# A four-layer graph attention kernel: the first head's G made by TensorE, and another order for first pieces, masks and elu

## The chip, the cores and the metric

The kernel runs on one core of one Trainium2 chip. The core has a matrix engine (TensorE, in the profile PE, with its weight loads as PEld), a vector engine (VectorE, DVE), a scalar engine (ScalarE, ACT), a general engine (GpSimd, POOL), and a queue of transfers that SyncE issues (SP). Each runs its own list of instructions in order and waits for the others through semaphores. The metric is the device time of one execution, in microseconds (us).

## The reference

The input x has 16 batch entries of 1024 nodes with 256 features, and adj is one 1024 x 1024 graph for all of them. Four layers follow one another, each of the form x = x + gnn(relu(layernorm(x))). Layers 0 and 2 have four heads of 64 features, layers 1 and 3 have one head of 256. For one head, cut to what matters:

```python
h    = relu(layernorm(x));  wh = h @ W
e    = leaky_relu(wh @ a_src [:, None] + wh @ a_dst [None, :])   # slope 0.2, in layer 3 0.01
e    = where(adj > 0 (layers 0, 1) or adj != 0 (layers 2, 3), e, -inf)
x    = x + elu(softmax(e) @ wh)                                   # layer 3: relu
```

## The kernel before, in words

**Algebra.** The exponential of a leaky relu of a sum is a maximum of two products, each with one factor by row and one by column. So no 1024 x 1024 exponential is computed. With a factor G for the node that receives and a factor r for the node that sends, DVE makes the unnormalised weights of 128 senders against all 1024 receivers in one instruction: w = max(G, r) * mask (`weights`, L355). G has to stand in PSUM as a row of 1024 values, the same on all 128 partitions. The other factors are folded into wh (`project`, L314), and one more column of wh gives the softmax denominator.

**Steps.** One layer of one batch entry is a step; there are 64. Four entries are under way at a time (streams), and the order of steps (`order_of_steps`) alternates four-head and one-head steps, except at the two ends: steps 0, 1 and 2 all have four heads, steps 5 and 6 are both of one head, 59 and 60 are both of four heads, and 61, 62 and 63 of one.

**What a step does.** Its preparation (`preparation`) is a list of 21 pieces:

- 0 to 4: statistics on DVE (L238), their combination on POOL (L265 to L277), normalisation on ACT (L283).
- 5 to 16: for each half of the nodes, transposes on PE (L291) with relu on ACT (L292), and projections on PE (L302), each evicted from PSUM by ACT (L304). The fourth of each half is followed by exponentials (L310, L312) and the fold on POOL (L314).
- 17 `factors`: gcol, the G of each node, by two ACT instructions (L320, L321).
- 18 `rows`: PE turns gcol into rows (L326), ACT copies them (L328), and SP writes them to DRAM (grow).
- 19 `fetch_heads`: SP reads a head's row back from DRAM into gs on all 128 partitions (L344). Two gs buffers are there.

Just before it is needed, `broadcast` copies gs into PSUM by ACT (L350). Then come 8 weights instructions per head, and the aggregation on PE (`aggregate`, L371) in 8 groups per step: in a four-head step a group is 128 matmuls of width 65, in a one-head step 16 of width 257. ACT evicts each group (L386). 18 buffers hold w. PSUM banks for projections, transposes and groups come from one pool of four, in turn.

`finish` closes a step: the reciprocal of the denominators (`divide`), scaling and the min of elu (`scaled`), the exponential on ACT (L420), and the sum into x (L426 on DVE, L427 on POOL). In `scaled` POOL multiplies (L414). The min is done by DVE ahead of it (L413) where the next step has one head, else by POOL behind it (L416).

**What sets the order.** The program order is written out by the kernel itself. Time is counted in slots, eight per step, one per group. The lists FOUR, SHORT, ONE, SOON, FIRST, TIGHT and LATE give the slot of each of the 21 pieces relative to a step's start. At each slot the main loop emits the group, then those pieces of the previous step's finish that are due (list `at`), then due preparation pieces, then weights ahead of time. `free` is the slot in which the stream's x is ready again. An engine does its instructions in this order, so an instruction that waits holds all behind it on its engine.

**The start.** The adjacency arrives as int32 rows in eight blocks. DVE turns a block into signs (L194), PE transposes it into PSUM (`turn`, L208), DVE writes the mask of layers 0 and 1 (`positive`, L211), and ACT the mask of layers 2 and 3 as a square (`nonzero`, L215). Blocks 0 to 3 share PSUM tiles in pairs, out of the pool that G uses later. A list named `order` mixes these pieces with step 0's preparation.

Of the kernel before, what the change touches and what calls it, by code (L numbers as in the profile page):

```python
# [35 lines left out]
P = 128  # L36
EPS = 1e-5
SHIFT = 60.0
STREAMS = 4
# [8 lines left out]
FOUR = (-8, -8, -5, -3, -2, -1, -1, 0, 0, 0, 0, 0, 0, 2, 2, 2, 2, 3, 8, 8, 10)  # L48
SHORT = (-4, -4, -4, -2, -2, -1, -1, 0, 0, 0, 0, 0, 0, 2, 2, 2, 2, 3, 8, 8, 10)
ONE = (2, 2, 2, 4, 4, 5, 5, 6, 6, 6, 6, 6, 6, 8, 8, 8, 8, 8, 10, 10, 12)  # L50
SOON = (0, 0, 0, 1, 2, 3, 3, 4, 4, 5, 5, 5, 5, 6, 6, 7, 7, 8, 9, 9, 11)
FIRST = (-4, -4, -4, -2, 0, -1, -1, -1, -1, -1, -1, 1, 1, 2, 2, 2, 2, 2, 3, 3, 5)
TIGHT = (5, 5, 5, 7, 7, 8, 8, 9, 9, 9, 9, 9, 9, 10, 10, 10, 10, 10, 11, 11, 13)
LATE = (0, 0, 0, 1, 1, 2, 2, 3, 3, 3, 3, 3, 3, 4, 4, 4, 4, 5, 6, 6, 8)


# [9 lines left out]
def kernel(ctx: ExitStack, tc: tile.TileContext, x, adj, ws, avs, out):  # L66
# [273 lines left out]

    def fetch(n, h):

        gs = state[n]["gs", h] = work.tile([P, N], F32, name="gs", bufs=2)
        nc.sync.dma_start(out=gs, in_=state[n]["grow"][h].rearrange("c i -> (c i)")  # L344
                          .partition_broadcast(P))

    def broadcast(n, h):

        g = state[n]["g", h] = ps_g.tile([P, N], F32, name="g")
        nc.scalar.activation(g, state[n]["gs", h], AF.Copy)  # L350

    def weights(n, h, jc):
# [6 lines left out]
    def aggregate(n, h, i0, per):  # L359
# [25 lines left out]
            return  # L385
        nc.scalar.activation(st["y"][:, i0:i0 + per, h, :], acc, AF.Copy)  # L386

    def finish(n):

        b, l = steps[n]  # L390
        H = LAYERS[l][0]
        D = F // H
        st = state[n]

        def views(half):
            s = slice(half * HALF, (half + 1) * HALF)
            return (xs[b][:, s, :].rearrange("p c (h d) -> p (c h) d", h=H),
                    st["y"][:, s, :, 0:D].rearrange("p c h d -> p (c h) d"),
                    st["r"][:, s, :].rearrange("p c h -> p (c h)"))

        def divide():
            st["r"] = small.tile([P, C, H], F32, name="r")
            nc.vector.reciprocal(st["r"], st["y"][:, :, :, D])

        def scaled(half):
            xh, yh, r = views(half)
            rb = r[:, :, None].to_broadcast([P, HALF * H, D])
            time = LAYERS[steps[n + 1][1]][0] == 1
            if l < L - 1:

                e = st["e", half] = prep.tile([P, HALF * H, D], F32, name="e")
                if time:
                    nc.vector.scalar_tensor_tensor(e, yh, 0.0, rb, op0=ALU.min, op1=ALU.mult)  # L413
            nc.gpsimd.tensor_tensor(yh, yh, rb, op=ALU.mult)  # L414
            if l < L - 1 and not time:
                nc.gpsimd.tensor_scalar(e, yh, 0.0, -3.0e38, op0=ALU.min, op1=ALU.max)  # L416

        def exponential(half):
            if l < L - 1:
                nc.scalar.activation(st["e", half], st["e", half], AF.Exp)  # L420

        def add(half):
            xh, yh, r = views(half)
            if l < L - 1:
                e = st["e", half]
                nc.vector.scalar_tensor_tensor(e, e, -1.0, yh, op0=ALU.add, op1=ALU.max)  # L426
                nc.gpsimd.tensor_add(xh, xh, e)  # L427
                return
            nc.vector.scalar_tensor_tensor(xh, yh, 0.0, xh, op0=ALU.max, op1=ALU.add)  # L429

        def store(half):
            nc.sync.dma_start(
                out=out[b].rearrange("(p c) f -> p c f", p=P)[:, half * HALF:(half + 1) * HALF],
                in_=xs[b][:, half * HALF:(half + 1) * HALF, :])
            if half == 1 and b + STREAMS < B:
                load(b + STREAMS)


        at = (0, 0, 0, 0, 1, 1, 1) if H > 1 else (0, 0, 1, 1, 2, 2, 3)
        return list(zip(at, (divide, lambda: scaled(0), lambda: scaled(1), lambda: exponential(0),  # L440
                             lambda: exponential(1), lambda: add(0), lambda: add(1)))) + (
                    [(4, lambda: store(0)), (4, lambda: store(1))] if l == L - 1 else [])
# [15 lines left out]
    def prepare(upto):  # L458

        while agenda and agenda[0][0] <= upto:  # L460
            _, n, piece, last = agenda.pop(0)
            piece()
            if last:
                done["prepared"] = n + 1
# [37 lines left out]
    last, agenda_of = {}, []  # L502
    for n, (b, l) in enumerate(steps):

        free = 8 * (last[b % STREAMS] + 1) + (8 if l == 0 else 2) if b % STREAMS in last else -99
        last[b % STREAMS] = n
        start = 8 * (n - 2) + (n == 3)
        kind = (ONE if n < len(steps) - 2 else TIGHT) if LAYERS[l][0] == 1 else SOON if n < 5 else FOUR
        if kind is FOUR and free > start + kind[0]:
            kind = SHORT  # L510
        if free > start + kind[0]:
            kind = LATE
            start = max(free, agenda_of[-1][0] + 5, start - LATE[7])
        agenda_of.append([start + k for k in kind] if n > 1 else FIRST)
        if n > 2:

            assert agenda_of[n][7] >= 8 * (n - 2)
            was = agenda_of[n - 1]
            assert agenda_of[n][3] >= was[5] and agenda_of[n][4] >= was[11]
    ending = []  # L520
    later = {}
    with tc.manual_schedule():
        blocks = [mask_rows(c) for c in range(C)]
        layer = [weight_columns(l) for l in range(L)]
        layer[0][0](nc.scalar)
        load(0, 2)
        load_weights(0)
        for c in range(C):
            blocks[c][0]()
        load(1)  # L530
        load_weights(1)
        for i in range(2, STREAMS):
            load(i)
        nc.scalar.activation(warm, half1, AF.Exp)
        nc.vector.tensor_copy(identb, ident)
        layer[0][1]()
        first = [piece for _, piece in preparation(0)]

        order = (

            [first[0], first[1], first[3], lambda: layer[0][2](range(1)), first[2],
             lambda: layer[0][2](range(1, K)), first[5], first[6], first[4], layer[0][3]]

            + [blocks[c][1] for c in range(4)]
            + [first[7], first[8], blocks[0][2], blocks[4][1], blocks[5][1], blocks[0][3],
               first[9], first[10], blocks[1][2], blocks[0][4], blocks[6][1], blocks[7][1],
               blocks[1][3], first[11], first[12], blocks[2][2], blocks[1][4],
               lambda: prepare(-4), first[13], first[14], blocks[3][2], blocks[2][4],
               blocks[2][3], blocks[3][3], first[15], first[16]]

            + [first[17], blocks[4][2], blocks[5][2], first[18], first[19],
               blocks[4][3], blocks[3][4], blocks[4][4], blocks[5][3], blocks[5][4],
               blocks[6][2], blocks[7][2], blocks[6][3], blocks[6][4], blocks[7][3], blocks[7][4]])
        plan(1)
        planned = 2
        for piece in order:
            piece()
        done["prepared"] = 1
        emit_tiles(C // 2, must=True)
        prepare(-2)  # L560
        emit_tiles(C, must=True)
        prepare(-1)
        for i in range(2, STREAMS):
            load_weights(i)

        for l, at in ((1, 1), (2, 8 * 3 + 3), (3, 8 * 5 + 3)):
            for i, piece in zip((0, 1, 2, 8), layer[l]):
                later[at + i] = piece
        for n in range(len(steps)):
            for k, (h, i0, per) in enumerate(groups(n)):  # L570
                while planned < len(steps) and min(
                        a[0] for a in agenda_of[planned:planned + 2]) <= 8 * n + k:
                    plan(planned)
                    planned += 1
                emit_tiles(place[n, h, C - 1] + 1, must=True)
                aggregate(n, h, i0, per)
                if i0 + per == C:
                    done["free"] = place[n, h, C - 1] + 1
                while ending and ending[0][0] <= k:
                    ending.pop(0)[1]()  # L580
                upto = min(done["tiles"] + (6 if per > 1 else 3), done["free"] + WBUFS)
                emit_heads(upto - 1)
                if 8 * n + k in later:
                    later[8 * n + k]()
                prepare(8 * n + k)
                emit_tiles(upto)
            for _, piece in ending:
                piece()
            ending = finish(n) if n < len(steps) - 1 else []
# [35 lines left out]
```

## Time and profile before

| what | us |
|---|---|
| median of 3 runs (lowest, highest) | 2562.08 (2561.59, 2566.2) |
| span of the profiled execution | 2559.7 |
| TensorE busy | 2497.2 |
| VectorE busy | 2018.9 |
| ScalarE busy | 1130.0 |
| GpSimd busy | 1110.1 |
| first weights instruction (L355) begins | 37.96 |
| step 3's aggregation begins | 201.19 |

A line of the summary gives an engine's busy time, its share of the span and the number of its instructions. In a line of the order of time, the columns are start, duration, engine, line, operation, written tile <- read tiles, and in brackets how long the engine stood idle before and which instruction released it. In a line of the waits they are who waited <- for whom: total, number, longest. A busy PE is not PE at its peak, since matmuls are pipelined.

### The profile page before, as it was taken

The numbers are of one execution on the slowest core, as the hardware profiler recorded it, in microseconds if no ns is written. First come the engines' busy times: TensorE is split into PE (matmuls) and PEld (weight loads), VectorE is DVE, ScalarE is ACT, GpSimd is POOL, SyncE is SP. The second block draws the span as 40 slices with busy tenths as digits, with TensorE's granted clock in tenths as the row PEclk, the third lists the DMA queues.
The fourth block names the chain that finished last, engine by engine and source line by source line (L and its number), as shares of the span: only waits on it lengthen the run. The fifth ranks groups of instructions, "written<-read, shape, count | busy, mean of one in ns | idle before, by whom it ended". The sixth has DMA issues, their size and how long they took to land.

```text
span 2559.7 us, 88174 instructions
## 1 busy us (share of the span) xinstructions
PE 2497.2 (98%) x40088; PEld 2258.7 (88%) x40088; DVE 2018.9 (79%) x2140; ACT 1130.0 (44%) x2502; POOL 1110.1 (43%) x1364
## 2 busy tenths in 40 slices
PE   6899999999999999999999999999999999999899
PEld 5788889999989999989999889999888999998887
DVE  8888578888778888778888778888778878778863
ACT  5344454434444444544434544444444444543331
POOL 3244455533444544544433545543443444544341
PEclk8999999999999999999999999999999999999999
DMA  5101010121212110111221101111212210111101
GB/s 182 52 28 41 12 43 35 44 77 44 76 42 70 44 44 11 43 41 71 77 76 44 43 35 44 44 44 43 75 37 76 76 36 19 43 35 43 61 10 58
DMA packets 36991, 129.01 MB, mean 50 GB/s; under 512 B 6278, under 2 KB 9094, under 8 KB 34696
## 3 DMA queue, kind: packets, MB, share of 16 engines
q1 hardware_dynamic: 36606, 123.36, 13.7%
q8 instruction: 314, 5.14, 0.8%
q14 instruction: 61, 0.50, 0.1%
q10 hardware_dynamic: 10, 0.00, 0.0%
HBM read 105.91 MB, written 17.43 MB: 48 GB/s over the span
## 4 chain that ended last, share of the span: by engine, by line
PE 84%; DVE 9%; POOL 3%; issue 2%; ACT 2%; DMA 0%; DVEq 0%; POOLq 0%; ACTq 0%
PE bank L371 63%; PE bank L302 17%; DVE w L355 7%; PE bank L291 4%; DVE bn L238 1%; ACT xn L283 1%; POOL x L427 1%; POOL rstd L271 1%; DVE e L426 0%; PE bank L326 0%; POOL y L414 0%; DVE e L413 0%; POOL e L416 0%; ACT g L350 0%; DMA x<-in_x 0%
## 5 line engine op out<-in xcount | busy, mean ns | idle before, releaser
L371 PE MATMUL bank<-whx,w 128*64 128x65 f32 x36864 | 1909.5, 241 | 29.3 <-DVE w L355 17.6
L371 PEld LDWEIGHTS bank<-whx,w 128*64 128x64 f32 x36864 | 1745.1, 145 | 174.3 <-DVE w L355 24.3
L355 DVE SCALAR_TENSOR_TENSOR w<-g,rcol,mask 128x1024 f32<-128x1024 f32 x1280 | 1540.2, 1272 | 392.1 <-PE bank L371 314.3
L386 ACT ACTIVATE y<-bank 128x260 f32<-128x260 f32 (+1 forms) x504 | 193.9, 385 | 1090.9 <-PE bank L371 1090.9
L414 POOL TENSOR_TENSOR y<-y,r 128x1024 f32<-128x1024 f32 x126 | 263.4, 2100 | 579.7 <-DVE e L413 448.6
L314 POOL TENSOR_TENSOR whx<-whx 128x1024 f32<-128x1024 f32 x128 | 257.5, 2012 | 583.9 <-ACT whx L312 583.9
L302 PE MATMUL bank<-wx,hT 128*128 128x264 f32 (+1 forms) x2048 | 482.2, 388 | 5.6 <-ACT y L386 4.4
L302 PEld LDWEIGHTS bank<-wx,hT 128*128 128x128 f32 x2048 | 382.7, 191 | 76.2 <-ACT y L386 14.4
L427 POOL TENSOR_TENSOR x<-x,e 128x1024 f32<-128x1024 f32 x96 | 247.9, 2593 | 136.1 <-DVE e L426 135.0
L283 ACT ACTIVATE xn<-x,shift,rstd 128x256 f32<-128x256 f32 x512 | 264.6, 590 | 73.2 <-POOL shift L277 71.2
L304 ACT ACTIVATE whx<-bank 128x264 f32<-128x264 f32 (+1 forms) x512 | 188.7, 384 | 178.3 <-PE bank L302 177.8
L238 DVE BATCH_NORM_STATS2 bn<-x 128x6 f32<-128x256 f32 x512 | 175.9, 411 | 79.5 <-POOL x L427 76.2
L426 DVE SCALAR_TENSOR_TENSOR e<-e,y 128x1024 f32<-128x1024 f32 x96 | 154.1, 1623 | 37.3 <-ACT e L420 30.0
L350 ACT ACTIVATE g<-gs 128x1024 f32<-128x1024 f32 x160 | 163.6, 1023 | 12.1 <-DVE w L355 9.7
L291 PE MATMUL bank<-ident,xn 128*128 128x128 f32 x1024 | 137.9, 277 | 10.5 <-ACT xn L283 10.3
L291 PEld LDWEIGHTS bank<-ident,xn 128*128 128x128 f32 x1024 | 120.8, 142 | 27.7 <-ACT xn L283 14.6
L292 ACT ACTIVATE hT<-bank 128x512 f32<-128x512 f32 x256 | 136.7, 585 | 1.4 <-PE bank L291 1.2
L271 POOL TENSOR_TENSOR rstd<-rstd,neghalf 128x4 f32<-128x4 f32 (+1 forms) x97 | 120.2, 1239 | 15.1 <-DVE shift L272 7.6
L420 ACT ACTIVATE e<-e 128x1024 f32<-128x1024 f32 x96 | 100.7, 1049 | 23.4 <-POOL e L416 23.1
L413 DVE SCALAR_TENSOR_TENSOR e<-y,r 128x1024 f32<-128x1024 f32 x60 | 72.5, 1250 | 2.2
L429 DVE SCALAR_TENSOR_TENSOR x<-y,x 128x1024 f32<-128x1024 f32 x30 | 44.9, 1499 | 2.0 <-POOL y L414 2.0
L312 ACT ACTIVATE whx<-whx,nbias 128x16 f32<-128x16 f32 (+1 forms) x128 | 40.2, 314 | 4.2
(63 smaller groups left out, 442.1 us busy)
## 6 DMA issues: line engine op xcount, KB each, us to landing
gs<-grow SPq DMA_DIRECT2D x160, 512.0 KB
x<-in_x SPq DMA_DIRECT2D x15, 1024.0 KB
out<-x SPq DMA_DIRECT2D x30, 512.0 KB
w<-in_adj SPq DMA_DIRECT2D x8, 512.0 KB
x<-in_x SPq DMA_DIRECT2D x2, 512.0 KB
wx<-in_L_gnn_W SPq DMA_DIRECT2D x8, 128.0 KB
out<-x SPq DMA_DIRECT2D x8, 128.0 KB
grow<-gT SPq DMA_DIRECT2D x32, 16.0 KB
```

What stands on the lines that cost most here:

```text
L238: nc.vector.bn_stats(bn[:, c, :], xs[b][:, c, :])
L283: nc.scalar.activation(xn[:, q, :], xs[b][:, c, :], AF.Identity, bias=st["shift"][:, c:c + 1], scale=st["rstd"][:, c:c + 1])
L291: nc.tensor.transpose(pt[:, q, :], st["xn", half][:, q, k * P:(k + 1) * P], ident)
L302: nc.tensor.matmul(pw, lhsT=st["hT", half][:, k, q * P:(q + 1) * P], rhs=wx[l][:, k, :], start=(k == 0), stop=(k == K - 1))
L304: nc.scalar.activation(st["whx"][:, c, :], pw, AF.Copy)
L314: nc.gpsimd.tensor_tensor(wh[:, :, :, 0:D], wh[:, :, :, 0:D], wh[:, :, :, D:D + 1].to_broadcast([P, HALF, H, D]), op=ALU.mult)
L350: nc.scalar.activation(g, state[n]["gs", h], AF.Copy)
L355: nc.vector.scalar_tensor_tensor(w, state[n]["g", h], state[n]["rcol"][:, jc, h:h + 1], masks[LAYERS[steps[n][1]][3]][:, jc, :], op0=ALU.m ...
L371: nc.tensor.matmul(acc[o % P:o % P + cols, q, :], lhsT=st["w", h, jc][:, o:o + cols], rhs=st["whx"][:, jc, h * (D + 1):(h + 1) * (D + 1)], ...
L386: nc.scalar.activation(st["y"][:, i0:i0 + per, h, :], acc, AF.Copy)
L414: nc.gpsimd.tensor_tensor(yh, yh, rb, op=ALU.mult)
L427: nc.gpsimd.tensor_add(xh, xh, e)
```

## The change

Five things are changed together.

1. The first head of step 0 gets its G from PE: eight transposes of a column of gcol, read as 128 equal columns, straight into PSUM. Its load from DRAM and its copy by ACT are left out.
2. In the list of first pieces, the squares of a pair of blocks come after both masks of the pair, step 0's first G comes ahead of the later blocks, and step 1's preparation is taken up earlier.
3. `slack` tells whether the next step has one head. The late form of `finish` is now also used where a four-head step follows a four-head step (it was for one-head steps alone); a one-head step always leaves the min of elu to POOL.
4. `free` is 4 rather than 2 slots into the next step where the late form is used before a four-head step.
5. The slots in SOON, FIRST and TIGHT move: factors and rows of the first steps by one slot, TIGHT by one, and TIGHT is chosen where the stream's x is late and no longer for the last two steps. Step 3 loses its extra slot. Of the slots, those of steps 0 to 4, 62 and 63 differ in the end.

```diff
-SOON = (0, 0, 0, 1, 2, 3, 3, 4, 4, 5, 5, 5, 5, 6, 6, 7, 7, 8, 9, 9, 11)
-FIRST = (-4, -4, -4, -2, 0, -1, -1, -1, -1, -1, -1, 1, 1, 2, 2, 2, 2, 2, 3, 3, 5)
-TIGHT = (5, 5, 5, 7, 7, 8, 8, 9, 9, 9, 9, 9, 9, 10, 10, 10, 10, 10, 11, 11, 13)
+SOON = (0, 0, 0, 1, 2, 3, 3, 4, 4, 5, 5, 5, 5, 6, 6, 7, 7, 7, 8, 8, 10)
+FIRST = (-4, -4, -4, -2, -0.9, -1, -1, -0.8, -0.8, -0.8, -0.8, 0, 0, 1, 1, 1, 1, 1, 2, 2, 4)
+TIGHT = (4, 4, 4, 6, 6, 7, 7, 8, 8, 8, 8, 8, 8, 9, 9, 9, 9, 9, 10, 10, 12)
...
     def fetch(n, h):
+        if n == 0 and h == 0:
+            return
...
     def broadcast(n, h):
         g = state[n]["g", h] = ps_g.tile([P, N], F32, name="g")
+        if n == 0 and h == 0:
+            for c in range(C):
+                nc.tensor.transpose(g[:, c * P:(c + 1) * P],
+                                    state[n]["gcol"][:, c, h:h + 1].to_broadcast([P, P]), ident)
+            return
...
+    def slack(n):
+        return LAYERS[steps[n + 1][1]][0] == 1
...
-                if time:
+                if H > 1 and slack(n):
                     nc.vector.scalar_tensor_tensor(e, yh, 0.0, rb, op0=ALU.min, op1=ALU.mult)
             nc.gpsimd.tensor_tensor(yh, yh, rb, op=ALU.mult)
-            if l < L - 1 and not time:
+            if l < L - 1 and not (H > 1 and slack(n)):
                 nc.gpsimd.tensor_scalar(e, yh, 0.0, -3.0e38, op0=ALU.min, op1=ALU.max)
...
-        at = (0, 0, 0, 0, 1, 1, 1) if H > 1 else (0, 0, 1, 1, 2, 2, 3)
+        at = (0, 0, 0, 0, 1, 1, 1) if slack(n) and H > 1 else (0, 0, 1, 1, 2, 2, 3)
...
-        free = 8 * (last[b % STREAMS] + 1) + (8 if l == 0 else 2) if b % STREAMS in last else -99
+            free = 8 * over + (8 if l == 0 else 2 if LAYERS[steps[over][1]][0] == 1 else 4)
-        start = 8 * (n - 2) + (n == 3)
-        kind = (ONE if n < len(steps) - 2 else TIGHT) if LAYERS[l][0] == 1 else SOON if n < 5 else FOUR
+        start = 8 * (n - 2)
+        kind = ONE if LAYERS[l][0] == 1 else SOON if n < 5 else FOUR
+        if kind is ONE and free > start + kind[0]:
+            kind = TIGHT
...
-               first[9], first[10], blocks[1][2], blocks[0][4], blocks[6][1], blocks[7][1],
-               blocks[1][3], first[11], first[12], blocks[2][2], blocks[1][4],
-               lambda: prepare(-4), first[13], first[14], blocks[3][2], blocks[2][4],
-               blocks[2][3], blocks[3][3], first[15], first[16]]
-            + [first[17], blocks[4][2], blocks[5][2], first[18], first[19],
-               blocks[4][3], blocks[3][4], blocks[4][4], blocks[5][3], blocks[5][4],
-               blocks[6][2], blocks[7][2], blocks[6][3], blocks[6][4], blocks[7][3], blocks[7][4]])
+               first[9], first[10], blocks[1][2], blocks[6][1], blocks[7][1], blocks[1][3],
+               first[11], first[12], blocks[2][2], blocks[0][4],
+               lambda: prepare(-4), first[13], first[14], blocks[1][4], blocks[2][3],
+               blocks[3][2], first[15], first[16], blocks[3][3]]
+            + [first[17], blocks[4][2], first[18], first[19], lambda: emit_heads(0),
+               blocks[5][2], blocks[6][2], blocks[4][3], blocks[4][4], blocks[5][3], blocks[5][4],
+               blocks[6][3], blocks[7][2], blocks[2][4], blocks[3][4], blocks[7][3],
+               lambda: prepare(-2), blocks[6][4], lambda: prepare(-1), blocks[7][4]])
-        emit_tiles(C // 2, must=True)
-        prepare(-2)
         emit_tiles(C, must=True)
-        prepare(-1)
+        prepare(-0.5)
```

In the diff blocks[c][1] to [4] are a block's signs, turn, mask and square, and first[i] is piece i of step 0.

More of the change, by code (lines that the diff above doesn't have):

```diff
@@ L407, in scaled @@
             rb = r[:, :, None].to_broadcast([P, HALF * H, D])
-            time = LAYERS[steps[n + 1][1]][0] == 1
             if l < L - 1:
                 e = st["e", half] = prep.tile([P, HALF * H, D], F32, name="e")
-                if time:
+                if H > 1 and slack(n):
                     nc.vector.scalar_tensor_tensor(e, yh, 0.0, rb, op0=ALU.min, op1=ALU.mult)
             nc.gpsimd.tensor_tensor(yh, yh, rb, op=ALU.mult)
-            if l < L - 1 and not time:
+            if l < L - 1 and not (H > 1 and slack(n)):
                 nc.gpsimd.tensor_scalar(e, yh, 0.0, -3.0e38, op0=ALU.min, op1=ALU.max)
@@ L503 @@
     for n, (b, l) in enumerate(steps):
-        free = 8 * (last[b % STREAMS] + 1) + (8 if l == 0 else 2) if b % STREAMS in last else -99
+        free = -99
+        if b % STREAMS in last:
+            over = last[b % STREAMS] + 1
+            free = 8 * over + (8 if l == 0 else 2 if LAYERS[steps[over][1]][0] == 1 else 4)
         last[b % STREAMS] = n
-        start = 8 * (n - 2) + (n == 3)
-        kind = (ONE if n < len(steps) - 2 else TIGHT) if LAYERS[l][0] == 1 else SOON if n < 5 else FOUR
+        start = 8 * (n - 2)
+        kind = ONE if LAYERS[l][0] == 1 else SOON if n < 5 else FOUR
         if kind is FOUR and free > start + kind[0]:
             kind = SHORT
+        if kind is ONE and free > start + kind[0]:
+            kind = TIGHT
         if free > start + kind[0]:
@@ L545 @@
             + [first[7], first[8], blocks[0][2], blocks[4][1], blocks[5][1], blocks[0][3],
-               first[9], first[10], blocks[1][2], blocks[0][4], blocks[6][1], blocks[7][1],
-               blocks[1][3], first[11], first[12], blocks[2][2], blocks[1][4],
-               lambda: prepare(-4), first[13], first[14], blocks[3][2], blocks[2][4],
-               blocks[2][3], blocks[3][3], first[15], first[16]]
-            + [first[17], blocks[4][2], blocks[5][2], first[18], first[19],
-               blocks[4][3], blocks[3][4], blocks[4][4], blocks[5][3], blocks[5][4],
-               blocks[6][2], blocks[7][2], blocks[6][3], blocks[6][4], blocks[7][3], blocks[7][4]])
+               first[9], first[10], blocks[1][2], blocks[6][1], blocks[7][1], blocks[1][3],
[6 more added lines that the diff above has]
+               lambda: prepare(-2), blocks[6][4], lambda: prepare(-1), blocks[7][4]])
         plan(1)
         planned = 2
+        done["prepared"] = 1
         for piece in order:
             piece()
-        done["prepared"] = 1
-        emit_tiles(C // 2, must=True)
-        prepare(-2)
         emit_tiles(C, must=True)
-        prepare(-1)
+        prepare(-0.5)
         for i in range(2, STREAMS):
```

## The prediction

> **What bounds the kernel now.** I read the summary first, then busy time by stage, then who TensorE (PE) waits for in the two poor stages, then the order of time inside them.
>
> ```profile
> PE 2497.2 (98%) x40088; PEld 2258.7 (88%) x40088; DVE 2018.9 (79%) x2140; ACT 1130.0 (44%) x2502; POOL 1110.1 (43%) x1364
> ```
>
> PE is the bound, so a gain can only come from its idle time, 2559.7 - 2497.2 = 62.5 us, and from a low clock. By stage (us, then busy time of PE, PEld, DVE, ACT, POOL, then granted clock):
>
> ```profile
> 0.00:46.00 46.00, 28.33 (x143) 20.88 (x143) 33.41 (x68) 27.23 (x49) 13.80 (x28) 0.89 0.70 252
> 46.00:201.00 155.00, 138.37 (x3251) 127.27 (x3250) 134.41 (x138) 62.30 (x133) 50.77 (x63) 0.92 0.10 34
> 201.00:2380.00 2179.00, 2168.47 (x34671) 1967.70 (x34671) 1739.41 (x1813) 987.36 (x2201) 987.89 (x1193) 1.00 0.14 48
> 2380.00:2454.00 74.00, 61.98 (x1572) 57.15 (x1567) 66.66 (x67) 25.69 (x55) 27.66 (x48) 0.97 0.12 38
> 2454.00:2560.00 106.00, 100.00 (x465) 85.69 (x463) 44.97 (x58) 27.46 (x66) 29.97 (x32) 0.98 0.11 40
> ```
>
> The long middle is full. What can be won lies in steps 0 to 2 (three four-head steps running) and at 2380 to 2454 (steps 59 and 60, both of four heads): there DVE is nearly full too, and PE idles. PE's waits at 60 to 250 us, then from 2380:
>
> ```profile
> PE bank L326 <- ACT gcol L321: 6.3, 1, 6.3
> PE bank L371 <- DVE w L355: 5.4, 7, 0.9
> PE bank L371 <- ACT whx L304: 2.7, 1, 2.7
> ...
> PE bank L371 <- DVE w L355: 7.1, 12, 0.9
> PE bank L371 <- ACT whx L304: 4.8, 1, 4.8
> ```
>
> The 6.3 us, in order of time: step 0's elu holds ScalarE (ACT), step 2's gcol stands behind it, and PE's L326 behind that. DVE waits for the same exponential.
>
> ```profile
> 110.55 1.04 POOL L416 TENSOR_SCALAR e<-y 128x1024 f32<-128x1024 f32 x1
> 111.63 1.06 ACT L420 ACTIVATE e<-e 128x1024 f32<-128x1024 f32 x1 [8.48 <-POOL e L416]
> 112.59 0.31 ACT L320 ACTIVATE gcol<-whx,cbias 128x32 f32<-128x32 f32 x1
> 112.71 1.83 DVE L426 SCALAR_TENSOR_TENSOR e<-e,y 128x1024 f32<-128x1024 f32 x1 [1.94 <-ACT e L420]
> 113.30 0.39 PE L326 MATMUL bank<-ident,gcol 128*32 128x128 f32 x1 [6.31 <-ACT gcol L321]
> ```
>
> The same at the end, on DVE: it idles 1.94 and 5.37 us between w tiles that PE needs.
>
> ```profile
> 2411.35 2.37 DVE L355 SCALAR_TENSOR_TENSOR w<-g,rcol,mask 128x1024 f32<-128x1024 f32 x2
> 2415.66 1.83 DVE L426 SCALAR_TENSOR_TENSOR e<-e,y 128x1024 f32<-128x1024 f32 x1 [1.94 <-ACT e L420]
> 2422.86 1.22 DVE L426 SCALAR_TENSOR_TENSOR e<-e,y 128x1024 f32<-128x1024 f32 x1 [5.37 <-ACT e L420]
> 2424.00 19.15 DVE L355 SCALAR_TENSOR_TENSOR w<-g,rcol,mask 128x1024 f32<-128x1024 f32 x16
> 2445.70 7.22 DVE L355 SCALAR_TENSOR_TENSOR w<-g,rcol,mask 128x1024 f32<-128x1024 f32 x6
> ```
>
> **The skill.** "PSUM — Partial Sum Buffer", section on bank collisions: two engines that touch one bank are put in order, two readers too. The trace agrees: a DVE mask waited 1.7 us for ACT's square. "Trainium Architecture — The Big Picture", section on one NeuronCore: each engine has its own instruction stream and they meet at semaphores; the queue gcol stood in is that. "TensorE: Matmul & The Clock Gate", Part 1: idling lowers PE's clock for a few us; at 100 to 120 us the trace has 0.74, and 280 matmuls that take 8.4 us elsewhere took 10.73. "DMA: Bandwidth & Descriptors", anatomy of one DMA: some 2.0 us fixed; here the 16 KB grow at 30.94 let its reader issue at 32.84, 1.9 us.
>
> **The change, part by part.** Figures are us of this execution; I follow each engine's new instruction order with the durations above.
>
> *First pieces and first G.* Removed: gs load and L350 copy of head 0 (1.03), with DVE's 3.26 idle from 34.70 to 37.96. Added: 8 PE transposes from gcol, priced by L291 (8 in 1.04, 2.80 cold; I take 1.1). Mask 1 no longer waits for a square (1.5 earlier), but PE's turn of block 3 now waits for mask 2, which stands behind 2.70 of statistics; behind that turn are the last projections and gcol. So: mask 1 at 22.0 to 23.2, statistics to 25.9, mask 2 to 27.0, turn 3 to 27.7, projections (2.0) to 29.7, L326 1.76 after them as before at 31.5, G to 32.7, turn 5 to 33.3, three masks (1.2 each) to 36.9. First w at 36.95 for 37.96: 1.0 won; bounds -1.5 and +3. The squares slide behind: ACT starts step 1's xn at 37.6 (37.87 before), and PE's first aggregate stays near 46.3.
>
> *Steps 0 to 2.* DVE made the 72nd w (last of step 2's first head) at 146.5. Its waits in between go: 6.19 for step 1's G at 82.9 (its gcol comes a slot earlier, so L350 copies it at 76.8 and no longer at 88.0), and 1.94 + 2.02 for the exponentials, now issued a slot later, with DVE's adds behind other w. 146.5 - 1.0 - 10.15 = 135.4. PE no longer stops 6.3 at L326 (gcol is a slot earlier). It runs unhindered to about 111, then waits for w as before, some 4 us in each of two groups, and ends that group at 135.4 + 3.1 = 138.5. From there PE is the bound: to the end of step 2 it has seven groups of 3.97 (27.8), 16 projection chunks of steps 3 and 4 at 0.95 (15.2), three sets of transposes (2.9), L326 (0.3), and 0.9 left of the 2.7 wait for L304, where step 1's first exponential still goes ahead of the evictions: 47.1, so 185.6. I add 2.9 for slow clock after the two stalls: 188.5. Step 3 began at 201.2: 12.7 won. Bounds 6 and 16.
>
> *A wait added.* SP now issues all four G loads of step 4 ahead of layer 2's vector a; the third and fourth wait for ACT's copies, the vector issues about 16.2 into step 3 and PE's L147 is due at 17.9. Landing takes 1.9 (grow) to 4.1 (G), so PE, with all that stands behind L147, waits 0 to 2.4: 1.0.
>
> *Elu of step 5 on POOL.* Takes 2 x 1.22 from DVE, adds 2 x 1.04 on POOL; its exponentials are issued later than both: nothing. Steps 8 to 58 keep their order on every engine: nothing.
>
> *Steps 59 to 63.* In the late schedule the four projection evictions no longer stand behind the exponential: PE's 4.8 goes. DVE: recip at 2411.2, w to 2413.8, 1.4 waiting for buffers, then w, elu, w, elu, w to 2434.8, statistics 2.7, step 61's eight w to 2447.1 for 2452.9. Counted where both orders have done the same, after step 61's second group: 2456.8 (1.0 of slow clock in it) for 2463.9: 7.1 won. Steps 62 and 63 are prepared one and three slots earlier: their first groups, which w held to 4.8 where a group takes 3.47, get 1.3 each: 2.6.
>
> Sum: 12.7 - 1.0 + 7.1 + 2.6 = 21.4; I take 1.4 off for half-microsecond waits that a replay by hand misses: 20. The execution shown spans 2559.7 and took 2561.5; the median of the runs is 2562.1. So 2542.
>
> **Rivals.** *Half of it* (2551): DVE sets the pace in both stages, and its w run longer beside POOL (mean 1272 for 1203 ns here; 70 ns x 64 = 4.5), with the first w late (38.5, 1.5 more) and new short waits: 10 to 12 left. For it: DVE is 87% busy at 46 to 201. Against: the waits removed are DVE's own.
> *No change* (2561): each wait turns into another on the same chain, ACT behind POOL. Against: the exponentials are now issued a whole group of 4 us later.
> *Slower* (2570): the middle. Its 28 pairs of steps take 76.7 or 77.2 us, nine of them with a wait of 0.5 of L302 for ACT's y. An earlier start shifts DMA landings and ACT's copies against PE; over 0.7 lost in each pair (20 in all) it eats everything, at 1.0 it gives 2570. Against: the order there is unchanged and only the phase moves.
>
> **How the numbers follow.** Likeliest 0.70, half 0.19, no change 0.06, slower 0.05. About 0.2% (5 us) is what a measurement here tells from no change, so faster 0.89, same 0.07, slower 0.04. The likeliest's own range: gains of 14 to 28, so 2534 to 2548. For 8 in 10 it must take in most of the half: 2533 to 2555.
>
> **What would show it.** First w near 37; no wait of L326 for gcol at 100 to 110; step 3's first 257-wide group near 188; PE's wait for whx L304 down to about 1 in steps 0 to 2 and gone at the end; step 61's w done near 2435 (2447.1 less 11.7 from the start); middle pairs still 76.7 to 77.2. Wrong if DVE still idles before the elu, if the first w comes after 39, or if the middle lengthens.

## The result and the profile after

| kernel | median us (lowest, highest, runs) | the kernel before beside it | ratio (95% interval) |
|---|---|---|---|
| changed | 2533.81 (2531.06, 2538.12, 4) | 2561.84 | 0.9891 (0.987 to 0.9911) |
| changed, again | 2531.44 (2529.93, 2533.61, 4) | 2561.79 | 0.9883 (0.9869 to 0.9898) |

The change makes the kernel 28 to 30 us faster (each row by its own kernel before); 20 were forecast (2542 us). The first profiled execution of the changed kernel spans 2536.3 us, the second (called "again" below) 2529.8; the kernel before spans 2559.7. First the summary of the changed kernel, then its busy time by stage (start and length in us, busy time of PE, PEld, DVE, ACT, POOL, granted clock, DMA share, GB/s):

```profile
PE 2489.7 (98%) x40096; PEld 2254.8 (89%) x40096; DVE 2014.6 (79%) x2138; ACT 1128.9 (45%) x2501; POOL 1106.6 (44%) x1366
```

```profile
46.00:188.00 142.00, 135.35 (x3220) 124.20 (x3217) 134.02 (x137) 62.07 (x134) 52.76 (x66) 0.99 0.12 38
188.00:2355.00 2167.00, 2152.39 (x34182) 1952.13 (x34181) 1721.49 (x1793) 982.15 (x2186) 979.68 (x1192) 1.00 0.14 48
2355.00:2430.00 75.00, 69.68 (x1986) 66.68 (x1984) 73.94 (x76) 26.54 (x55) 28.15 (x47) 0.98 0.17 53
2430.00:2537.00 107.00, 102.27 (x519) 89.04 (x514) 48.97 (x63) 29.61 (x71) 31.63 (x36) 1.00 0.11 40
```

PE idles 15.9 us less (62.5 before, 2536.3 - 2489.7 = 46.6 now) and is busy 7.5 us less. Steps 0 to 2 now end at 182.68, where step 3 begins, with the clock at 0.99; before they ended at 201.19 with the clock at 0.92. PE's waits, at 60 to 250 us and then from 2380 (who waits <- for whom: us, times, longest):

```profile
PE bank L379 <- DVE w L363: 5.2, 7, 0.9
PE bank L379 <- ACT whx L304: 1.5, 1, 1.5
PE bank L379 <- issue: 1.3, 2, 0.8
PE bank L147 <- DMA e<-in_L_gnn_a: 1.0, 1, 1.0
...
PE bank L379 <- DVE w L363: 2.1, 3, 0.9
```

The 6.3 us for gcol and the 4.8 for whx are gone. The same work now comes some 25 us earlier, so that from 2380 shows less of it than before: from 2355 on, the second execution has 4.3 us of waits for w in six pieces and one stop of 1.7 that nothing shown explains. In order of time, steps 0 and 1 (start, duration, engine, line, operation):

```profile
93.77 0.30 ACT L320 ACTIVATE gcol<-whx,cbias 128x32 f32<-128x32 f32 x1
96.53 0.28 PE L326 MATMUL bank<-ident,gcol 128*32 128x128 f32 x1
101.97 1.06 ACT L431 ACTIVATE e<-e 128x1024 f32<-128x1024 f32 x1 [0.84 <-POOL e L427]
105.44 1.05 ACT L431 ACTIVATE e<-e 128x1024 f32<-128x1024 f32 x1
108.56 1.22 DVE L437 SCALAR_TENSOR_TENSOR e<-e,y 128x1024 f32<-128x1024 f32 x1
112.08 1.27 DVE L437 SCALAR_TENSOR_TENSOR e<-e,y 128x1024 f32<-128x1024 f32 x1
```

gcol (93.77) now stands ahead of the exponentials on ACT, and PE's L326 follows it without a wait. DVE reaches its adds (L437) after the exponentials are done and waits for neither. The end, on DVE:

```profile
2403.48 7.25 DVE L363 SCALAR_TENSOR_TENSOR w<-g,rcol,mask 128x1024 f32<-128x1024 f32 x6 [0.54 <-PE bank L379]
2410.64 1.22 DVE L437 SCALAR_TENSOR_TENSOR e<-e,y 128x1024 f32<-128x1024 f32 x1
2411.77 2.47 DVE L363 SCALAR_TENSOR_TENSOR w<-g,rcol,mask 128x1024 f32<-128x1024 f32 x2
2414.16 1.24 DVE L437 SCALAR_TENSOR_TENSOR e<-e,y 128x1024 f32<-128x1024 f32 x1
```

The first and the third are runs of w; the two adds between and behind them wait for nothing, where DVE idled 1.94 and 5.37 us before.

### The profile page after: what moved, and what is told of

Same layout as the page of the kernel before. It is cut to its first block, busy times and chain, and to the rows that moved or that the text cites. A ratio compares the mean times of both kernels' runs of the same rounds, so it can differ in the third digit from the quotient of the medians.

```text
span 2536.3 us, 88187 instructions
## 1 busy us (share of the span) xinstructions
PE 2489.7 (98%) x40096; PEld 2254.8 (89%) x40096; DVE 2014.6 (79%) x2138; ACT 1128.9 (45%) x2501; POOL 1106.6 (44%) x1366
## 4 chain that ended last, share of the span: by engine, by line
PE 87%; DVE 7%; POOL 3%; issue 2%; ACT 1%; DMA 0%; DVEq 0%; SPq 0%; POOLq 0%; ACTq 0%
PE bank L379 65%; PE bank L302 17%; DVE w L363 5%; PE bank L291 4%; ACT xn L283 1%; POOL x L438 1%; DVE bn L238 1%; POOL rstd L271 1%; DVE e L437 0%; PE bank L326 0%; DVE e L424 0%; DVE wx L158 0%; DVE mask L211 0%; POOL shift L277 0%; DVE e L157 0%
## 5 line engine op out<-in xcount | busy, mean ns | idle before, releaser
L314 POOL TENSOR_TENSOR whx<-whx 128x1024 f32<-128x1024 f32 x128 | 259.2, 2025 | 561.9 <-ACT whx L312 561.9
L304 ACT ACTIVATE whx<-bank 128x264 f32<-128x264 f32 (+1 forms) x512 | 189.3, 385 | 178.4 <-PE bank L302 178.1
L437 DVE SCALAR_TENSOR_TENSOR e<-e,y 128x1024 f32<-128x1024 f32 x96 | 156.1, 1644 | 31.9 <-ACT e L431 22.8
L291 PEld LDWEIGHTS bank<-ident,xn 128*128 128x128 f32 x1024 | 119.8, 142 | 24.6 <-ACT xn L283 11.3
```

The source lines that it names most:

```text
L291: nc.tensor.transpose(pt[:, q, :], st["xn", half][:, q, k * P:(k + 1) * P], ident)
L304: nc.scalar.activation(st["whx"][:, c, :], pw, AF.Copy)
L314: nc.gpsimd.tensor_tensor(wh[:, :, :, 0:D], wh[:, :, :, 0:D], wh[:, :, :, D:D + 1].to_broadcast([P, HALF, H, D]), op=ALU.mult)
```

## Experiments

To compare traces I use, from the profiled executions: when DVE begins the 72nd w (the last of step 2's first head), when PE begins step 3's first group of width 257, and how far an execution is ahead of the kernel before when ACT copies the rows (L328) of steps 8 and 60, between which the orders are the same, and at its end. In the kernel before the first two are 146.49 and 201.19.

| kernel | 72nd w | step 3 | ahead at 8 | at 60 | at the end | ratio (95% interval) |
|---|---|---|---|---|---|---|
| changed | 131.38 | 182.68 | 16.5 | 10.8 | 23.4 | 0.9891 (0.987 to 0.9911) |
| again | 132.08 | 181.84 | 18.2 | 18.7 | 29.9 | 0.9883 (0.9869 to 0.9898) |
| late_only | 141.97 | 192.90 | 9.9 | 9.0 | 18.1 | 0.9936 (0.9922 to 0.9949) |
| no_late | 137.73 | 197.52 | 3.9 | 0.0 | 4.2 | 0.9979 (0.9971 to 0.9987) |
| old_slots | 137.51 | 187.27 | 13.9 | 8.9 | 21.5 | 0.9911 (0.9897 to 0.9924) |
| no_pe_g | 136.14 | 187.17 | 14.7 | 11.3 | 23.9 | 0.9898 (0.9884 to 0.9911) |
| old_first | 136.01 | 187.32 | 14.2 | 13.3 | 25.9 | 0.9912 (0.9898 to 0.9926) |
| old_ends | 131.73 | 183.04 | 18.6 | 18.7 | 26.9 | 0.991 (0.9896 to 0.9923) |

**The elu part alone (late_only), and all but the elu part (no_late).** The same lines, put into the kernel before and taken out of the changed one:

```diff
+                if H > 1 and slack(n):        # late_only: into the kernel before; no_late: the reverse
...
+        at = (0, 0, 0, 0, 1, 1, 1) if slack(n) and H > 1 else (0, 0, 1, 1, 2, 2, 3)
```

> The kernel before with the elu part of the change alone: where four heads follow four (steps 0, 1 and 59) the exponentials and adds are issued a slot or two later and the elu's minimum goes to POOL. First pieces, G of head 0, slots of the preparation stay as before. My theory (several separate waits, each on its own queue): at the end all of the 9.9 us that the new kernel won in steps 59 to 61 comes; at the start only DVE's two waits for the exponentials and the shorter adds, 4 to 6 us, since DVE's 6.2 us wait for step 1's G stays; PE's wait of L326 for gcol (6.3) goes, but PE then waits for w instead. Sum 14 to 16: 2546 to 2548. Rival 'elu alone' (slots and first pieces are hidden behind it): 22 to 28 won, 2534 to 2540. Rival 'the slots carry the start': nothing at the start, 10 at the end, 2552.

Measured 2545.31 us, 16.5 less than before. By the trace 9.9 came at the start, where 4 to 6 were expected, and 9.1 at the end (18.1 - 9.0), where 9.9 were. (The expectations of this run and the next speak of the minimum of the elu as moving to POOL or back to DVE. In steps 0, 1 and 59 POOL makes it in both kernels, L416 before and L427 after; only step 5's moves, and it was not tried alone.) DVE's waits from 40 us to the 72nd w:

```profile
DVE w L355 <- ACT g L350: 6.2, 1, 6.2
DVE bn L238 <- POOL x L430: 1.2, 1, 1.2
```

The 6.2 is step 1's G, as expected. The start gained more than DVE's 4.5 us (146.49 to 141.97). The stop for gcol has turned into waits for w, as expected (8.0 at 60 to 250 us for 5.4 before). But from the 72nd w to step 3 it takes 50.93 for 54.70: PE no longer stops 2.7 us for whx there, and its clock at 145 to 182 us is 1.00 for 0.95. The last 1.6 came behind step 3 (8.3 ahead there), where the clock at 260 to 300 us was 0.96 before and is 1.00 here.

> The new kernel with the elu part taken back: where four heads follow four, minimum on DVE and exponentials and adds in the slots of the kernel before; all else new. My theory: the 9.9 us of steps 59 to 61 are lost and PE waits about 5 us for whx L304 there again; at the start DVE waits for the exponentials again (4 to 6 us), while PE's wait of L326 for gcol (6.3 us before) does not come back, for gcol now stands a slot ahead of the exponential. 14 to 16 us more than the new kernel: 2546 to 2550. Rival 'elu alone': nearly all is lost, 2555 to 2562. Rival 'slots carry the start': 10 lost, 2543 to 2544.

Measured 2557.02: some 23 to 26 us lost against the changed kernel, not 14 to 16. DVE's 4.0 for the exponentials came back as expected, and gcol didn't; but a wait that I had not foreseen did:

```profile
153.32 1.97 PE L291 MATMUL bank<-ident,xn 128*128 128x128 f32 x8 [7.45 <-ACT whx L304]
151.94 1.06 ACT L432 ACTIVATE e<-e 128x1024 f32<-128x1024 f32 x1 [9.31 <-POOL e L428]
152.90 1.20 ACT L304 ACTIVATE whx<-bank 128x258 f32<-128x258 f32 x4
```

In the kernel before, in the same place:

```profile
152.04 0.39 ACT L304 ACTIVATE whx<-bank 128x258 f32<-128x258 f32 x1 [0.48 <-PE bank L302]
160.70 1.06 ACT L420 ACTIVATE e<-e 128x1024 f32<-128x1024 f32 x1 [3.50 <-POOL e L416]
```

Step 1's first exponential waits 9.31 for POOL, and step 3's four projection evictions (L304) stand behind it on ACT; PE's transposes need their PSUM bank and stop 7.45. In the kernel before the last of those evictions (152.04) came ahead of the exponential (160.70). So the other parts, with the elu as before, win 3.9 at the start: they need the late elu. The elu alone wins 9.9, and both together 18.2. At the end the 4.8 us wait for whx is back, and 4.2 of the gain remain (4.2 - 0.0).

**The slots of steps 1, 2 and 4 (old_slots).**

```diff
-SOON = (..., 7, 7, 7, 8, 8, 10)      FIRST = (..., 0, 0, 1, 1, 1, 1, 1, 2, 2, 4)
+SOON = (..., 7, 7, 8, 9, 9, 11)      FIRST = (..., 1, 1, 2, 2, 2, 2, 2, 3, 3, 5)
```

> The new kernel with the last slots of the two early preparations (steps 1 and 2, and step 4) one later again, as before; late elu, first pieces and first G stay new. My theory: step 1's G is copied a group later again, DVE waits some 6 us for it and, since DVE sets the pace from the first w to the 72nd, step 3 begins about 6 us later: 2538 to 2541. PE's wait of L326 for gcol does not come back, for the exponentials are now issued later than it. Rival 'elu alone': no change, within 1 us of the new kernel. Rival 'slots carry the start': 10 or more lost, 2544 or more.

Measured 2539.57, 5.8 above the changed kernel's first median and 8.1 above its second. The 72nd w is 5.4 to 6.1 later than in its two executions and PE's wait for gcol stays away, as expected. DVE's wait is nearly the whole of it:

```profile
DVE w L363 <- ACT g L358: 5.3, 1, 5.3
```

**The first G and the first pieces (no_pe_g, old_first).** no_pe_g loads the first head's G from DRAM and copies it by ACT, in the new order; old_first takes back the order as well.

```diff
+            lambda: emit_heads(0),     # no_pe_g: behind blocks[5][3]; gs by DMA, g by ACT's Copy
...
+            ...                        # old_first: list `order` and FIRST's first pieces as before
```

> The new kernel with the first head's G as before: written to DRAM, loaded to all partitions and copied to PSUM by ACT (the copy stands between the squares of the masks, after the load has landed); the new order of first pieces stays. My theory: the first w comes 1 to 2.6 us later and the whole start with it, since DVE sets the pace from there: 2534.5 to 2537. Rival 'the first G carries the start': 6 to 8 us lost, 2540 or more. Rival 'hidden': no change.

> The new kernel with the order of first pieces and the first head's G as in the kernel before (G by way of DRAM and a copy of ScalarE, squares between the masks), and with the new slots and the late elu. My theory: first pieces and first G together are worth 2 to 4 us (G alone was worth about 2.5): 2535.5 to 2538. Rival 'the new order of pieces is paid back by its wait of PE for mask 2': with the old order nothing more is lost than G's 2.5, or less: 2533.5 to 2536. Rival 'the first pieces carry the start': 8 or more lost, 2542 or more.

no_pe_g took 2536.28 beside 2561.79 for the kernel before, and old_first 2536.8 beside 2559.82. The first w, in no_pe_g, old_first and the changed kernel again:

```profile
39.23 1.28 DVE L355 SCALAR_TENSOR_TENSOR w<-g,rcol,mask 128x1024 f32<-128x1024 f32 x1 [3.10 <-ACT g L350]
```

```profile
37.00 1.28 DVE L355 SCALAR_TENSOR_TENSOR w<-g,rcol,mask 128x1024 f32<-128x1024 f32 x1 [2.95 <-ACT g L350]
```

```profile
36.04 2.48 DVE L363 SCALAR_TENSOR_TENSOR w<-g,rcol,mask 128x1024 f32<-128x1024 f32 x2
```

By the marks G from TensorE is worth some 4 us at the start (72nd w 136.14 to 132.08; 14.7 to 18.2 at step 8), and the order of pieces nothing that can be told (old_first: 136.01, 14.2). In time the ratios differ from the changed kernel's by 0.0007 to 0.0029, 2 to 7 us, with intervals that overlap or touch. In old_first the first w is only 1.0 later than in the changed kernel again, but DVE then waits 3.1 us for PE (for L170's matmuls and for L371's aggregation), where it waited 0.2. Neither the first G nor the pieces carry the start. Item 4 of the change and the extra slot of step 3 were not tried alone.

**Steps 62 and 63 (old_ends).**

```diff
-        start = 8 * (n - 2)
+        start = 8 * (n - 2) + (n > 61)           # and TIGHT for both
```

> The new kernel with the preparation of steps 62 and 63 in the slots of the kernel before (one slot later in 62, one to three later in 63). My theory: the groups around the end of steps 60 and 61 get back their w at the old pace, 2 to 3 us lost: 2536 to 2537. Rival 'hidden': no change within 1 us, since steps 59 to 61 already gave the slack. Everything ahead of step 60 is as in the new kernel, the jump of some 3 to 5 us near 1220 us too.

2535.69 beside 2559.82. At step 60 the execution is as far ahead as the changed kernel's second, and at the end 3.0 less: the slots are worth about 3, as expected, and the 8.2 left are the elu's. (Each put in without the other, the slots won 4.2, by no_late, and the elu 9.1, by late_only: more than the 11.2 of both.) PE's waits for w from 2402 on, of the changed kernel again and of old_ends, account for 2.0 of it:

```profile
PE bank L379 <- DVE w L363: 2.7, 4, 0.9
```

```profile
PE bank L379 <- DVE w L363: 4.7, 9, 0.9
```

**A loss in the middle (phase64, after_again).** In the first execution of the changed kernel 5.3 us went at 1220 to 1240, with PE idle for nothing that is shown, and a slow stretch behind it. The same work, in that execution and in the second:

```profile
1221.45 3.95 PE L379 MATMUL bank<-whx,w 128*64 128x65 f32 x128 [0.64 <-issue]
1227.95 12.11 PE L379 MATMUL bank<-whx,w 128*64 128x65 f32 x242 [2.54 <-issue]
```

```profile
1210.58 22.56 PE L379 MATMUL bank<-whx,w 128*64 128x65 f32 x656
```

The trace has PE's instructions fetched 5.4 and 6.7 us apart there, 3.6 to 4.0 in the second execution. To see whether the place in the instruction stream matters I moved it:

```diff
+        for i in range(64):                      # behind the first spread()
+            nc.tensor.matmul(dummy[0:1, i:i + 1], lhsT=ones[0:1, 0:1], rhs=ones[0:1, 0:1], ...)
```

> The new kernel with 64 one-element matmuls added on PE behind the first small matmul, in 2.9 us in which PE waits for ScalarE anyway; nobody reads them. They only move PE's instruction stream by 64 matmuls against the data transfers. The trace of the new kernel shows between 1213 and 1226 us two gaps of 5.4 and 6.7 us between the fetches of PE's instructions (some 3.7 apart elsewhere at that pace), with PE idle for nothing that is shown, and 5.3 us lost there against the kernel before; the kernel before and the one with the elu part alone have no such gap there. Theory 'fetch': the loss belongs to where a fetch of PE's instructions falls against the 2 MB of output and x moved at that moment; with the stream shifted by half a fetch, the jump at 1213 to 1226 us goes or moves: distance to the kernel before from the middle on steady within 1 us, time 2528 to 2532. Rival 'the new order makes the wait': the jump of 2.7 to 5.3 us stays at the same place, 2533 to 2536. Rival 'one execution': the jump is not there but the median is that of the new kernel, within 1 us.

> The new kernel once more, unchanged, beside the other three. Theory 'one execution': the 5.3 us lost at 1213 to 1226 us in its first profile are not there, the distance to the kernel before stays within 1 us from step 5 to step 58, at 18 to 19, and the span shown is 2528 to 2531. Theory 'the stream of this order meets the transfer': the jump of 2.7 to 5.3 us is at the same place again.

phase64: no jump, 2531.39 beside 2559.82, ratio 0.9891 (0.9878 to 0.9905). The changed kernel again: no jump either, so the order alone doesn't make it, and moving the stream gained nothing that can be measured. In the profiles of six other kernels 2.1 to 2.5 us went at the same place (no_late, old_slots, no_pe_g and the three with the elu's adds on POOL), in five others at most 0.3. What makes it, and whether late fetches are its cause or follow from it, stays open.

**The vector of layer 2 earlier (early_vec).**

```diff
-            for i, piece in zip((0, 1, 2, 8), layer[l]):
+            for i, piece in zip((-1 if l == 2 else 0, 1, 2, 8), layer[l]):
```

> The new kernel with the load of layer 2's vector a issued one slot earlier, ahead of the third and fourth G load of step 4 on SP. Expected: PE's wait of L147 for this load (0.9 to 1.0 us in the new kernel, at 201 us) goes, step 3's L326 and all behind it come 0.9 earlier; the time 0 to 1 us less, which these rounds can hardly tell from none. Rival: the third G load, now behind the vector, comes later than ACT's copy needs it: no gain or up to 1 us lost.

2531.11, ratio 0.9883 (0.9866 to 0.9899): the same. The wait of L147 is gone, and at step 8 it is ahead by 18.1, where the changed kernel again is by 18.2. PE's waits for w from 40 to 250 us:

```profile
PE bank L379 <- DVE w L363: 5.4, 8, 0.9
```

These are 5.2 in the first execution of the changed kernel and 4.4 in the second, so they don't tell where the 1.0 us went. The execution began step 3 at 183.09, 1.25 later than the changed kernel again, and its clock at 249 to 255 us was 0.72 for 1.00. No gain can be told, and whether the 1.0 us of L147 cost anything stays open.

**Elu's adds off DVE (pool_elu, pool_stats, best).** DVE looked like the bound of both stages, so these were tries for a faster version. pool_stats adds the later statistics to pool_elu, best adds the earlier vector and another order of two operations.

```diff
+                if H > 1 and not slack(n):
+                    nc.gpsimd.tensor_scalar(yh, yh, 0.0, -1.0, op0=ALU.max, op1=ALU.add)  # best: -1, then max -1
+                    nc.gpsimd.tensor_add(xh, xh, yh)
+                else:
                     nc.vector.scalar_tensor_tensor(e, e, -1.0, yh, op0=ALU.add, op1=ALU.max)
...
-TIGHT = (4, 4, 4, 6, 6, 7, ...)
+TIGHT = (4, 6, 6, 6, 7, 7, ...)                 # pool_stats, best
```

> The new kernel with the adds of the elu of steps 0, 1 and 59 taken from DVE: x + max(e - 1, y) is made by POOL as x + (max(y, 0) - 1) + e, one more tensor_scalar (1.0) and one more add (2.4) per half on POOL, 1.2 less per half on DVE. Theory 'DVE sets the pace in steps 0 to 2 and 59 to 61': the 72nd w comes 2 to 2.4 us earlier and step 61's w 1 to 2.4 earlier; 2 to 4 us less than the new kernel, 2529 to 2532. Rival 'PE has caught up': DVE's spare time changes nothing, within 1 us of the new kernel. Rival 'POOL': its longer chain and its traffic beside DVE's w cost more than they give: 2 us or more above the new kernel.

> The kernel with the adds of the elu of steps 0, 1 and 59 on POOL, and the second half of the statistics of steps 3 and 62 (with what hangs on it) two slots later, so that eight w stand ahead of it on DVE. In the version without this DVE waited 3.65 us at 120.8 and 3.2 us near 2419.3 for POOL's x in front of these statistics, and its 72nd w ended at 135.4. Theory 'the wait of the statistics took what DVE gained': the wait goes, the 72nd w ends 1.5 to 2.4 us earlier than the new kernel's 132.7 to 133.2; time 1 to 4 us less than the new kernel on the same chip. Rival 'PE is the bound from there': the 72nd w comes earlier, the time stays within 1 us of the new kernel's. Rival 'POOL costs more': 2 us or more above it.

> Both of the two edits just named together (elu's adds on POOL with the later statistics, and the earlier vector load), and POOL's max(y, 0) - 1 written as max(y - 1, -1), add first. That tensor_scalar took 3.66 us on POOL as max then add, where the one with min then max (other tile written) takes 1.04. Theory 'the order of the two operations costs it': 1.0 to 1.1 us now, and POOL is done with x some 5 us earlier. Rival 'writing y in place, rows of 65, costs it': still 3.6. Time: 2 to 5 us less than the new kernel if DVE sets the pace at both ends, within 1 us of it if PE does.

All had higher medians than the changed kernel: 2536.99 (0.991, 0.9896 to 0.9923), 2540.8 (0.9919, 0.9904 to 0.9933) and 2539.1 (0.9912, 0.9898 to 0.9927). For pool_elu and pool_stats the rival with POOL came in time, and best missed the 2 to 5 us less that were expected of it. In pool_elu the 72nd w begins 2.0 later than in the changed kernel again (134.10), not 2 to 2.4 earlier. The statistics of step 3 stand in DVE's queue before w and wait for POOL's x:

```profile
124.44 1.41 DVE L238 BATCH_NORM_STATS2 bn<-x 128x6 f32<-128x256 f32 x4 [3.65 <-POOL x L442]
113.71 2.37 POOL L442 TENSOR_TENSOR x<-x,e 128x1024 f32<-128x1024 f32 x1
116.05 3.65 POOL L438 TENSOR_SCALAR y<-y 128x1024 f32<-128x1024 f32 x1
122.04 2.36 POOL L442 TENSOR_TENSOR x<-x,e 128x1024 f32<-128x1024 f32 x1
```

In pool_stats that wait is gone and the 72nd w begins at 129.16, 2.9 earlier than in the changed kernel; but the normalisation of that half is now late, and PE waits for it, and for ACT behind it, at the start (in order of time) and from 2380 on (its waits):

```profile
128.74 0.33 PE L291 MATMUL bank<-ident,xn 128*128 128x128 f32 x1 [1.81 <-ACT xn L283]
129.23 2.31 PE L291 MATMUL bank<-ident,xn 128*128 128x128 f32 x7 [0.17 <-ACT xn L283]
137.99 3.80 PE L302 MATMUL bank<-wx,hT 128*128 128x258 f32 x16 [1.98 <-ACT hT L292]
```

```profile
PE bank L302 <- ACT hT L292: 3.8, 1, 3.8
PE bank L291 <- ACT xn L283: 2.7, 3, 2.4
```

DVE won 2.9 us, PE lost 4.0 at 128 to 138 and 6.5 at the end. DVE is not the only bound in these stages: the chain from statistics to projections is as tight. No version that I tried beats the changed kernel.

## Why the prediction was right, and where it was off

The case named likeliest came: several waits, each on its own queue, and the gain at the two ends. By the second execution of the changed kernel, which the next paragraphs use where they name no other, 2559.7 - 2529.8 = 29.9:

| term | forecast | measured | from |
|---|---|---|---|
| start, to step 3's first group | 12.7 | 19.35 | 201.19 - 181.84 |
| step 3 to step 58, L147 in it | -1.0 | -0.65 | 18.7 ahead at step 60's rows |
| steps 59 to 61 | 7.1 | 8.4 | 27.1 ahead after step 61's second group (2463.89 - 2436.75), less 18.7 |
| steps 62, 63 | 2.6 | 2.8 | 29.9 - 27.1; 3.0 by old_ends |
| allowance | -1.4 | 0 | |

The start is the term that was sized too small; the next paragraphs take it apart. The other executions of this order up to step 3 (the first, early_vec, old_ends and phase64) begin step 3 at 182.68 to 183.24, which makes 18.0 to 18.5.

**L147 (1.0).** The wait was 0.95 and 1.04, as worked out. What it cost in time is open, as early_vec shows no gain without it.

**First w (forecast 36.95).** 36.04: 0.9 better (35.32 to 35.90 in the four others). The wait of block 3's turn for mask 2 came as worked out, here in the first execution:

```profile
25.80 0.65 PE L208 MATMUL g<-identb,w 128*128 128x128 bf16 x8 [1.73 <-DVE mask L211]
30.16 1.04 PE L355 MATMUL g<-ident,gcol 128*128 128x128 f32 x8
```

The eight transposes took 1.04 for the 1.1 taken. What was mis-sized is the worth of G, and by the choice of comparison: I counted against the kernel before (1.0), whose load landed early enough. In the new order with the load kept, the first w was at 39.23.

**The 72nd w (135.4).** 132.08. Of the 3.3, 0.9 is the first w. 1.6 is the adds, which I left at their old length: before, 1.83 and 2.29; now 1.21 and 1.25. "SBUF — State Buffer", section on the two separate sides, says that a DVE instruction with two inputs in SBUF and a GpSimd one that reads SBUF take turns, each whole. The trace agrees: the add of 1.83 began at 112.71 while POOL's L414 ran until 113.46, and that of 2.29 while POOL added x; now POOL is idle when the first begins, and has 0.2 to go when the second does. The remaining 0.8 is of the same kind, overlooked in the forecast: the first multiplication of L157 took 1.14 beside POOL's L314, and takes 0.42 now that POOL is idle. In the kernel before:

```profile
70.53 1.89 POOL L314 TENSOR_TENSOR whx<-whx 128x1024 f32<-128x1024 f32 x1 [16.08 <-ACT whx L312]
71.57 1.14 DVE L157 TENSOR_TENSOR e<-wx,e 128x256 f32<-128x256 f32 x1
111.56 1.90 POOL L414 TENSOR_TENSOR y<-y,r 128x1024 f32<-128x1024 f32 x1
115.41 2.37 POOL L427 TENSOR_TENSOR x<-x,e 128x1024 f32<-128x1024 f32 x1
116.56 2.29 DVE L426 SCALAR_TENSOR_TENSOR e<-e,y 128x1024 f32<-128x1024 f32 x1 [2.02 <-ACT e L420]
```

**From there to step 3 (53.1).** 49.8. The 2.9 for slow clock did not come in this execution: the granted clock at 46 to 188 is 1.00. That is luck of the execution. At 130 to 140 us (granted clock, the third number from the end) the first execution, the second, and late_only have:

```profile
130.00:140.00 10.00, 7.97 (x120) 7.31 (x121) 10.00 (x10) 4.48 (x10) 0.00 (x0) 0.83 0.01 2
130.00:140.00 10.00, 7.71 (x140) 6.80 (x137) 10.00 (x9) 5.57 (x12) 0.00 (x0) 1.00 0.01 2
130.00:140.00 10.00, 7.39 (x119) 6.85 (x120) 10.00 (x10) 5.46 (x11) 1.85 (x5) 0.66 0.18 54
```

The three other executions of the new order have 0.83 too, and with the first they take 51.3 us from the 72nd w to step 3: 1.5 of the 2.9 came in four executions of five. I had PE wait some 4 us in each of two groups "as before", which misreads the kernel before (4.6 in all, at 120 to 140 us); now it waits 3.8, in five pieces of at most 0.9. "TensorE: Matmul & The Clock Gate", Part 1, gives a window of some 3.4 us of idling behind which PE is slowed, and tells of a kernel whose short but frequent idling did it too; the second is what these traces agree with. In late_only PE waits nine times at 100 to 140 us, 7.1 in all and never over 0.9, and the clock at 130 to 140 is 0.66. L304's wait was 1.4 for 0.9.

**The end.** Step 61's w ended at 2428.3; the replay's 2447.1 less the 18.7 by which the execution was ahead is 2428.4. The order was replayed rightly, and the term is short mainly by the 1.0 of slow clock that I put into it: the groups there took 3.64.

**The rivals.** *Half of it* fell: the first 72 w took 1.276 us each on the mean, 1.272 before, so that they did not get longer, and the first w came early. (Its 1203 ns is 9.62 us for eight w in a run, at 37.96, over eight: their distance, and not the length of one.) *No change* and *slower* fell with it: the distance to the kernel before went from 18.2 at step 8 to 18.7 at step 60 (in the first execution from 16.5 to 10.8, which still leaves 23.4 at the end). But the wait that takes the place of another was real: no_late shows it, 7.5 us. With the exponentials late the evictions stand ahead of it.

The first median, 2533.81, lies in the range of 2533 to 2555, near its low end, and the second, 2531.44, just below it; both are below the 2534 to 2548 given for the likeliest case. So the mechanism was right, and the range held in part by luck: two of the first four runs, 2531.06 and 2532.7, are outside it. The start was sized too small, 12.7 for 18.0 to 19.4.

## What to carry to other kernels

On in-order engines a wait is paid by whatever is queued behind it: find the instruction that waits, then move it behind those that others need, here the exponential behind gcol and the evictions. Edits to such an order don't add up: 9.9 us by one and 3.9 by the rest at the start made 18.2 together, so test each by taking it out of the whole as well as by putting it in alone. And an engine that looks like the bound is worth relieving only if no other chain is as tight: 2.9 us won on DVE became 9 us lost (2540.8 for 2531.44).

## What the hardware showed unexpectedly

POOL's tensor_scalar on y in place took 3.66 us (3.67 with the two operations in the other order), where L427, which reads the same y and writes e, took 1.04. So the order of operations isn't it, and DVE's work beside it isn't either: all 18 of these in pool_elu, pool_stats and best took 3.62 to 3.67, and L427 took 1.04 beside the same w. What is left, the place written (in place, in rows of 65) or the add that L427 doesn't have, was not tried. PE's granted clock was 0.66 over 10 us in late_only with no wait over 0.9 us; with such waits it was 0.83 in one execution of the changed kernel and 1.00 in another. And one execution can lose 5.3 us in one place, as the first profile of the changed kernel did: a second profile of the same kernel is worth having before a loss is explained.
